# Channel matrices of the later convolution slices completed on chip, and one input gate of the first step pair formed by seven products instead of eight

## The chip, the cores and the metric

The kernel runs on one NeuronCore of a Trainium2 chip. The metric is the device time of one execution in microseconds, as the median of three runs. The kernel is one launch; all five engines (TensorE = PE, VectorE = DVE, ScalarE = ACT, GpSimd = POOL, SyncE = SP) work from queues of their own, and each executes its queue in order.

## The reference, cut to what matters

The whole program is a GRU over 64 steps, a ternary-weight layer, a depthwise convolution over the batch axis and a mixture of experts with a shared expert. Only the GRU's input gates and the convolution are touched.

```python
x: (B=128, T=64, D=512)      cond_2048: (128, 512)
# 1 GRU
gi = x_t @ W_ih + b_ih;  gh = h @ W_hh + b_hh          # each (128, 1536): gates r, z, n
r = sigmoid(i_r + h_r); z = sigmoid(i_z + h_z); n = tanh(i_n + r * h_n)
h = (1 - z) * n + z * h
# 2 x = x + einsum(h, ternary(weight)) + bias
# 3 causal depthwise convolution along the 64 steps, a tap per channel and step, from cond_2048
y = conv(x, taps) + b
# 4 x = x + experts(y) + shared_expert(y)
```

All matrices are float32. Everything after step 3 is the same in both kernels.

## The kernel before

**Order of the work.** The scan of 64 steps comes first (0 to about 1398 us of the profile), then the convolution (about 1398 to 1467 us), then the shared expert with the routing and the experts. A scheduler places each instruction in its engine's queue from the order in which the Python code emits it; where the code needs a fixed order it says so with `in_order` (a chain of VectorE instructions) or `tc.issue_after`.

**Input gates.** `input_gates` is a generator: each `yield` stands for one product of two matmuls (128x256 outputs, contraction 2 x 128), and the scan's loop pulls ten or eleven of them into each step, between the step's recurrent products (`psgh`, line 598) and the turning of the new state. Steps are taken in pairs. For every pair but the first, a gate's two steps are computed by `Chunk` with seven products in place of eight: the operand sums of the pair (`pair_operands`, four GpSimd instructions of 128x256) and the weight sums (`prepare`, four VectorE instructions of 128x512 a gate) allow it, and VectorE adds the partial results with the bias. The third product of a chunk is executed within the following chunk. The first pair (t = 0 and 1) is computed in the plain way by `first_products`: for each gate 2 x 2 blocks for two steps, eight yields, four ScalarE copies out of PSUM. Gates come in the order 0, 2, 1. Their biases are added afterwards by `first_biases`, VectorE instructions in the fixed chain. The products pulled ahead of the first recurrent product are 24 of the first pair, then the turning of the initial state, then three of the second pair.

**Channel matrices.** A slice `sl` of the convolution has 32 channels (two halves `hf` of DS = 16). For each channel the convolution is a matrix of taps: `tz[partition 2s+hf, hf, u, d, t]` holds, for step s, output half u and channel d, the tap `s + 32u + t`. `toeplitz(q)` writes the matrices of one group of 16 channels from `taps` to DRAM (`tzd`) during step q + 2 of the scan, one DMA for each output half: u = 0 has only the 32 steps s = 32 to 63, u = 1 all 64. `load_toeplitz(sl)` brings a slice's matrices to SBUF by four DMAs: two of 64 KB (u = 0) and two of 128 KB (u = 1). For the first NCB = 4 slices SP issues them, within the scan; for slices 4 to 15 GpSimd issues them, within the convolution. There are four `tz` buffers and four `xc` buffers (`sl % NCB`), so the loads of slice sl wait until TensorE has done slice sl - 4.

**Convolution.** Per slice SP also issues two loads of 512 KB of the activations (`load_steps`, `xc<-x1c`). A slice is four groups of eight matmuls (`conv_group`, line 182, 16 records of the profile a group), and VectorE adds the bias while it moves each group to `hid` (line 713, two instructions a group). The last slices are followed by the stores of the expert table and the loads of the shared expert's weights.

Of the kernel before, what the change touches and what calls it, by code (L numbers as in the profile page):

```python
# [8 lines left out]
F32 = mybir.dt.float32  # L9
# [10 lines left out]
P = 128  # L20
# [22 lines left out]
def adaln_ffn_kernel(  # L43
# [22 lines left out]
    nc = tc.nc  # L66
# [8 lines left out]
    tzd = dram.tile([2 * NSL, 2, T, DS, T // 2], F32, name="tzd")  # L75
# [10 lines left out]
        out=before,  # L86
        in_=before,
# [18 lines left out]
    tzs, xcs = [], []  # L106
# [15 lines left out]
    NCB = 4  # L122
# [6 lines left out]
    HALVES = [(0, T // 2), (1, 0)]  # L129

    def toeplitz(q):


        for u, s0 in HALVES:
            i = nc.sync.dma_start(
                out=tzd[q, u, s0:],
                in_=bass.AP(
                    taps.tensor,
                    taps.offset + q * DS * 2 * T + s0 + u * T // 2,
                    [[1, T - s0], [2 * T, DS], [1, T // 2]],  # L140
                ),
            )
            tc.keep_in_program_order(i)

        nc.sync.dma_start(
            out=x1c[q, :TAIL].rearrange("s (r b) e -> (s r) (b e)", r=8), in_=zrow[: 8 * TAIL, : B * DS // 8]
        )

    def load_toeplitz(sl):
        for hf in range(2):
            for u, s0 in HALVES:
                (nc.sync if sl < NCB else nc.gpsimd).dma_start(
                    out=tzs[sl % NCB][2 * s0 + hf :: 2, hf, u], in_=tzd[2 * sl + hf, u, s0:]
                )

    def load_steps(sl, steps):
        for hf in range(2):
# [36 lines left out]
    HK = KD // 2  # L196
    HD = D // 2
    gis_ = ExitStack()
    ps_gi = gis_.enter_context(tc.tile_pool(name="ps_gi", bufs=1, space=PSUM))
    with (  # L200
# [9 lines left out]
        xps, xns = {}, {}  # L210
# [30 lines left out]
        bi = wi.tile([P, 3 * D], F32, name="bi")  # L241
# [12 lines left out]
        cols = [slice(c * D, (c + 1) * D) for c in range(3)]  # L254
# [24 lines left out]
        bh = {}  # L279
# [21 lines left out]
        ps = ps_f.tile([P, D], F32, name="psf")  # L301
# [7 lines left out]
        def prepare(c):  # L309

            w11, w12, w21, w22 = (block(c, k, n) for k in range(2) for n in range(2))
            t1, t2, t4 = (wi.tile([P, HK, HD], F32, name=f"t{n}{c}") for n in (1, 2, 4))
            in_order(nc.vector.tensor_sub, t1, w12, w11)
            in_order(nc.vector.tensor_sub, t2, w22, t1)
            in_order(nc.vector.tensor_sub, w12, w22, w12)
            in_order(nc.vector.tensor_sub, t4, w21, t2)
            wsum[c] = {1: w11, 2: w21, 3: w22, 4: t4, 5: t1, 6: t2, 7: w12}
# [3 lines left out]
        def in_order(op, *operands):  # L321
            with tc.issue_after(summed[-1].ins) if summed else nullcontext():
                summed.append(op(*operands))

        def first_biases(t):
            for c in (0, 2, 1):
                b = bi[:, cols[c]]
                if t == 0 and c in bh:
                    in_order(nc.vector.tensor_add, b, b, bh[c])
                in_order(nc.vector.tensor_add, gis[t, c], gis[t, c], b)  # L330

        def first_products(c, xp):

            for t in range(2):
                gis[t, c] = gip.tile([P, 2, HD], F32, name="gi").rearrange("p h d -> p (h d)")
            accs = {}
            for k in range(2):
                for n in range(2):
                    for t in range(2):
                        if k == 0:  # L340
                            accs[t, n] = ps_gi.tile(
                                [P, D], F32, name={(0, 0): "psx", (1, 0): "psw", (0, 1): "psy", (1, 1): "psz"}[t, n]
                            )[:, :HD]
                        for j in range(HK):
                            i = nc.tensor.matmul(
                                accs[t, n],
                                xp[:, t, k * HK + j, :],
                                block(c, k, n)[:, j, :],
                                start=(k == 0 and j == 0),
                                stop=(k == 1 and j == HK - 1),  # L350
                            )
                        made.append(i)
                        if k == 1:
                            nc.scalar.copy(gis[t, c][:, n * HD : (n + 1) * HD], accs[t, n])
                        yield
# [5 lines left out]
        def pair_operands(t):  # L361

            xp = xps.pop(t)
            x11, x12 = xp[:, 0, :HK], xp[:, 0, HK:]
            x21, x22 = xp[:, 1, :HK], xp[:, 1, HK:]
            s = xpp.tile([P, 3, HK, B], F32, name="xs")
            s1, s2, s4 = s[:, 0], s[:, 1], s[:, 2]
            engine = nc.gpsimd
            engine.tensor_add(s1, x21, x22)
            engine.tensor_sub(s2, s1, x11)  # L370
            engine.tensor_sub(x21, x11, x21)
            engine.tensor_sub(s4, x12, s2)
            return {1: x11, 2: x12, 3: s4, 4: x22, 5: s1, 6: s2, 7: x21}

        class Chunk:


            def __init__(self, t, c, ops):
                self.c, self.ops, self.ws = c, ops, wsum[c]
                self.g = [gip.tile([P, 2, HD], F32, name="gi") for _ in range(2)]  # L380
                gis[t, c], gis[t + 1, c] = (g.rearrange("p h d -> p (h d)") for g in self.g)
                self.ps = {}

            def product(self, n):

                name, first = {
                    1: ("psx", True),
                    2: ("psx", False),
                    6: ("psy", True),
                    7: ("psw", True),  # L390
                    4: ("psw", False),
                    5: ("psz", True),
                    3: ("psz", False),
                }[n]
                if first:
                    self.ps[name] = ps_gi.tile([P, D], F32, name=name)[:, :HD]
                ps = self.ps[name]
                for k in range(HK):
                    i = nc.tensor.matmul(  # L399
                        ps,  # L400
                        self.ops[n][:, k, :],
                        self.ws[n][:, k, :],
                        start=(first and k == 0),
                        stop=(k == HK - 1),
                        skip_group_check=not first,
                    )
                made.append(i)
                g0, g1 = self.g
                add = nc.vector.tensor_add
                both = ps.unsqueeze(1).to_broadcast([P, 2, HD])  # L410
                b = bi[:, cols[self.c]].rearrange("p (h d) -> p h d", h=2)
                if n == 1:
                    self.p1 = gtp.tile([P, 2, HD], F32, name="p1")
                    add(self.p1, both, b)  # L414
                elif n == 6:
                    self.u2 = gtp.tile([P, 2, HD], F32, name="u2")
                    add(self.u2, both, self.p1)
                elif n == 7:
                    self.u3 = gtp.tile([P, HD], F32, name="u3")
                    add(self.u3, ps, self.u2[:, 1])  # L420
                elif n == 5:
                    add(g1[:, 1], ps, self.u3)
                elif n == 2:
                    add(g0[:, 0], ps, b[:, 0])
                elif n == 4:
                    add(g1[:, 0], ps, self.u2[:, 0])
                elif n == 3:
                    add(g0[:, 1], ps, self.u2[:, 1])

        def input_gates():  # L430


            prev = None
            xp = xps.pop(0)
            for c in (0, 2, 1):

                for _ in first_products(c, xp):
                    yield
                if c == 0:
                    prepare(0)  # L440
            prepare(2)
            first_biases(0)
            prepare(1)
            first_biases(1)
            for t in range(2, T, 2):
                ops = pair_operands(t)
                for c in (0, 2, 1):
                    cur = Chunk(t, c, ops)
                    for n in (1, 6, 7, 3, 2, 4, 5):
                        which = prev if n == 3 else cur  # L450
                        if which:
                            which.product(n)
                            yield
                    prev = cur
            prev.product(3)
            yield
# [66 lines left out]

        stream = input_gates()
        load_x(0)
        for _ in range(24):
            next(stream)
        hT = transposed(h)
        for _ in range(3):
            next(stream)  # L530

        def ternary():
# [1131 lines left out]
```

## Time and profile before

| | |
|---|---|
| median of 3 runs | 2639.47 us (2638.37 to 2640.01) |
| the profiled execution's own time | 2639.73 us |
| its span (first to last instruction) | 2637.7 us |
| TensorE busy | 2626.6 us, so idle for 11.1 us of the span |
| VectorE, ScalarE, GpSimd busy | 1403.7, 427.7, 451.4 us |
| granted TensorE clock | 1.0 throughout |
| convolution, 1398 to 1475 us | TensorE busy 72.99 of 77.00 us, DMA engines busy 95%, 319 GB/s |

The profiled execution is 0.26 us over the median of the runs, and 2.03 us of it lie outside its span. The share of busy time of an engine is an average; what bounds a stage is read from that stage: from the windows' table, the gaps of TensorE in its timeline, and the landing times of the transfers.

### The profile page before, as it was taken

The numbers are of one execution on the slowest core, as the hardware profiler recorded it, in microseconds if no ns is written. First come the engines' busy times: TensorE is split into PE (matmuls) and PEld (weight loads), VectorE is DVE, ScalarE is ACT, GpSimd is POOL, SyncE is SP. The second block draws the span as 40 slices with busy tenths as digits, with TensorE's granted clock in tenths as the row PEclk, the third lists the DMA queues.
The fourth block names the chain that finished last, engine by engine and source line by source line (L and its number), as shares of the span: only waits on it lengthen the run. The fifth ranks groups of instructions, "written<-read, shape, count | busy, mean of one in ns | idle before, by whom it ended". The sixth has DMA issues, their size and how long they took to land.

```text
span 2637.7 us, 31178 instructions
## 1 busy us (share of the span) xinstructions
PE 2626.6 (100%) x11993; PEld 1826.7 (69%) x11993; DVE 1403.7 (53%) x3110; ACT 427.7 (16%) x795; POOL 451.4 (17%) x512
## 2 busy tenths in 40 slices
PE   9999999999999999999999999999999999999999
PEld 7666666666666666666668767878877666666667
DVE  6555555555555555555557755666675343333434
ACT  1111111111111111111110222222221111111111
POOL 2111121111111111111113100000001222222220
PEclk9999999999999999999999999999999999999999
DMA  5333232332322222322228831222255999999972
GB/s 197 73 58 66 54 63 59 58 61 54 61 47 52 44 52 44 76 44 52 44 57 278 303 90 21 44 62 63 70 161 158 304 304 283 283 314 301 292 203 50
DMA packets 477492, 323.33 MB, mean 123 GB/s; under 512 B 329056, under 2 KB 397920, under 8 KB 475168
## 3 DMA queue, kind: packets, MB, share of 16 engines
q1 hardware_dynamic: 448880, 248.18, 33.9%
q0 software_dynamic: 28464, 73.16, 11.5%
q8 instruction: 95, 1.56, 0.2%
q14 instruction: 53, 0.43, 0.0%
HBM read 235.01 MB, written 92.55 MB: 124 GB/s over the span
## 4 chain that ended last, share of the span: by engine, by line
PE 99%; DMA 1%; DVE 0%; issue 0%; POOL 0%; ACT 0%; SPq 0%; DVEq 0%
PE psgh L598 25%; PE psw L823 7%; PE psz L823 7%; PE psx L823 7%; PE psz L399 6%; PE psw L399 6%; PE psx L399 6%; PE psf L494 4%; PE y L823 4%; PE py L1549 3%; PE psy L399 3%; PE pg L1523 3%; PE pu L1523 3%; PE y L1000 2%; PE psc L182 1%; PE lg L1151 1%
## 5 line engine op out<-in xcount | busy, mean ns | idle before, releaser
L598 PE MATMUL psgh<-whh,hT 128*128 128x512 f32 x1528 | 671.0, 595 | 0.5 <-ACT hT L471 0.5
L598 PEld LDWEIGHTS psgh<-whh,hT 128*128 128x128 f32 x1528 | 285.2, 190 | 348.5 <-issue 334.6
L399 PE MATMUL psx<-wih,xp 128*128 128x256 f32 x744 | 191.0, 379 | 0.0
L220 POOL DMA_DIRECT2D xn<-in_x_dram x61 | 33.9, 555 | 841.3 <-DVE x L506 828.9
L399 PEld LDWEIGHTS psx<-wih,xp 128*128 128x128 f32 x744 | 138.9, 190 | 18.0 <-issue 0.5
L625 DVE TENSOR_TENSOR n<-psgh,bhn 128x512 f32<-128x512 f32 (+1 forms) x65 | 44.3, 683 | 171.0 <-PE psgh L598 170.9
L1533 DVE SCALAR_TENSOR_TENSOR a<-a,rw,pu 128x352 f32<-128x352 f32 x32 | 18.6, 580 | 213.0 <-PE pu L1523 213.0
L471 ACT COPY hT<-psf 128x512 f32<-128x512 f32 x63 | 37.0, 587 | 556.5 <-PE psf L463 556.4
L609 DVE TENSOR_TENSOR r<-psgh,gi 128x512 f32<-128x512 f32 x64 | 44.3, 692 | 141.2 <-PE psgh L598 141.2
L1105 POOL DMA_DIRECT2D out_dram<-hid x32 | 27.6, 1010 | 449.8 <-issue 332.9
L490 POOL TENSOR_TENSOR xn<-xn,fb 128x512 f32<-128x512 f32 x61 | 77.0, 1263 | 143.7 <-DMA xn<-in_x_dram 143.7
L399 PE MATMUL psz<-wih,xs 128*128 128x256 f32 x372 | 95.6, 379 | 0.1
L399 PE MATMUL psw<-t,xp 128*128 128x256 f32 x372 | 95.6, 379 | 0.0
L399 PE MATMUL psy<-t,xs 128*128 128x256 f32 x372 | 95.5, 379 | 0.0
L399 PE MATMUL psz<-t,xs 128*128 128x256 f32 x372 | 95.5, 379 | 0.0
L494 PE MATMUL psf<-sgn,hhi 128*128 128x512 f32 x256 | 95.1, 493 | 0.3 <-DVE hlo L479 0.3
L399 PE MATMUL psw<-wih,xp 128*128 128x256 f32 x372 | 95.4, 379 | 0.0
L1549 PE MATMUL py<-wd,aeT 128*64 128x512 f32 (+1 forms) x384 | 88.8, 597 | 0.0
L628 ACT ACTIVATE n<-n 128x512 f32<-128x512 f32 (+1 forms) x65 | 40.4, 623 | 276.7 <-DVE n L627 276.7
L414 DVE TENSOR_TENSOR p<-psx,bi 128x512 f32<-128x512 f32 x93 | 64.4, 692 | 36.9 <-PE psx L399 36.9
L1523 PE MATMUL pg<-wg,xeT 128*64 128x352 f32 x512 | 81.2, 459 | 0.0
L1523 PE MATMUL pu<-wu,xeT 128*64 128x352 f32 x512 | 81.2, 459 | 0.0
(350 smaller groups left out, 4760.2 us busy)
## 6 DMA issues: line engine op xcount, KB each, us to landing
wg<-in_w_gate_dram SPq DMA_DIRECT2D x64, 704.0 KB, 12.5
wu<-in_w_up_dram SPq DMA_DIRECT2D x64, 704.0 KB, 12.6
wd<-in_w_down_dram SPq DMA_DIRECT2D x64, 512.0 KB, 9.8
x1c<-x SPq DMA_DIRECT2D x62, 256.0 KB, 5.2
out_dram<-x SPq DMA_DIRECT2D x62, 256.0 KB, 5.4
xn<-in_x_dram POOLq DMA_DIRECT2D x61, 256.0 KB, 4.1
xp<-in_xT_dram POOLq DMA_DIRECT2D x30, 512.0 KB, 5.2
xc<-x1c SPq DMA_DIRECT2D x28, 512.0 KB, 8.6
```

The lines of the kernel that those rows point to most:

```text
L399: i = nc.tensor.matmul(ps, self.ops[n][:, k, :], self.ws[n][:, k, :], start=(first and k == 0), stop=(k == HK - 1), skip_group_check=not f ...
L414: add(self.p1, both, b)
L490: nc.gpsimd.tensor_add(xn, xn, fb)
L494: nc.tensor.matmul(ps, piece[:, k, :], sgn[:, k, :], start=(i == 0 and k == 0), stop=(i == 1 and k == KD - 1),)
L598: nc.tensor.matmul(ps[:, piece], hT[:, k, :], whh[c][:, k, piece], start=(k == 0), stop=(k == KD - 1),)
L609: i = nc.vector.tensor_add(r, ps_r, gis.pop((t, 0)))
L625: nc.vector.tensor_add(n[:, p], ps_n[:, p], bhn[:, p])
L628: nc.scalar.activation(n[:, p], n[:, p], AF.Tanh)
L823: i = nc.tensor.matmul(ps.rearrange("p (j b) -> p j b", b=P) if len(r.shape) == 3 else ps, lhs(k), r, start=(first and k == 0), stop=(k == ...
L1000: nc.tensor.matmul(gu.rearrange("p (j b) -> p j b", b=P), swr[:, k].rearrange("p w n -> p (w n)"), rows[:, k], start=(k == 0), stop=(k == ...
L1523: nc.tensor.matmul(acc[halves[j]], self.xeT[:, k, halves[j]], self.ws[j][which][:, k, :], start=(k == 0), stop=(k == KD - 1),)
L1549: nc.tensor.matmul(py[halves[j]], self.aeT[:n, c, halves[j]], self.ws[j][2][:n, c, :], start=(c == 0), stop=(c == len(ech) - 1),)
```

## The change

It has two parts.

**First part.** The matrix of u = 0 on partitions 64 to 127 (steps 32 to 63) equals that of u = 1 on partitions 0 to 63 (steps 0 to 31). For slices 4 to 15 the u = 0 half is no longer written to `tzd` (24 DMAs of SP less in the scan) and no longer loaded (24 DMAs of GpSimd less in the convolution). In its place ScalarE copies it within the buffer, 64 partitions x 1024 elements, once a slice.

**Second part.** Gate 1 of the first pair is computed by a `Chunk` of seven products, with operand sums by GpSimd for pair 0. The chunk leaves its biases out (`biased=False`): product 1 and product 2 leave PSUM by ScalarE copies, and `first_biases` adds all biases of the first pair once the chunk's product 3 is done. Since the plain products of the two other gates still need x21, the operand `x11 - x21` of pair 0 goes to a buffer of its own. `prepare(1)` moves ahead of `prepare(2)`. Ahead of the first recurrent product there are now 22 products, the turning of the initial state, and four products.

```diff
     def toeplitz(q):
-        for u, s0 in HALVES:
+        for u, s0 in HALVES if q < 2 * NCB else HALVES[1:]:
...
     def load_toeplitz(sl):
+        tz = tzs[sl % NCB]
         for hf in range(2):
             for u, s0 in HALVES:
-                (nc.sync if sl < NCB else nc.gpsimd).dma_start(
-                    out=tzs[sl % NCB][2 * s0 + hf :: 2, hf, u], in_=tzd[2 * sl + hf, u, s0:]
-                )
+                if sl < NCB or u:
+                    (nc.sync if sl < NCB else nc.gpsimd).dma_start(
+                        out=tz[2 * s0 + hf :: 2, hf, u], in_=tzd[2 * sl + hf, u, s0:]
+                    )
+        if sl >= NCB:
+            nc.scalar.copy(tz[P // 2 :, :, 0], tz[: P // 2, :, 1])
...
         def first_biases(t):
             for c in (0, 2, 1):
-                b = bi[:, cols[c]]
-                if t == 0 and c in bh:
-                    in_order(nc.vector.tensor_add, b, b, bh[c])
-                in_order(nc.vector.tensor_add, gis[t, c], gis[t, c], b)
+                in_order(nc.vector.tensor_add, gis[t, c], gis[t, c], bi[:, cols[c]])
...
+            s7 = x21 if t else gtp.tile([P, 2, HD], F32, name="p1")[:, 0].rearrange(
+                "p (k b) -> p k b", k=HK
+            )
-            engine.tensor_sub(x21, x11, x21)
+            engine.tensor_sub(s7, x11, x21)
...
                 if n == 1:
                     self.p1 = gtp.tile([P, 2, HD], F32, name="p1")
-                    add(self.p1, both, b)
+                    if self.biased:
+                        add(self.p1, both, b)
+                    else:
+                        for h_ in range(2):
+                            nc.scalar.copy(self.p1[:, h_], ps)
...
+                elif n == 2 and not self.biased:
+                    nc.scalar.copy(g0[:, 0], ps)
...
         def input_gates():
             prev = None
-            xp = xps.pop(0)
-            for c in (0, 2, 1):
+            xp = xps[0]
+            ops = pair_operands(0)
+            for c in (0, 2):
                 for _ in first_products(c, xp):
                     yield
                 if c == 0:
                     prepare(0)
+                    prepare(1)
+            cur = Chunk(0, 1, ops, False)
+            for n in (1, 6, 7, 2, 4, 5):
+                cur.product(n)
+                yield
+            prev = cur
             prepare(2)
-            first_biases(0)
-            prepare(1)
-            first_biases(1)
+            for c in (0, 1):
+                in_order(nc.vector.tensor_add, bi[:, cols[c]], bi[:, cols[c]], bh[c])
...
                             which.product(n)
+                            if not which.biased and n == 3:
+                                for t_ in range(2):
+                                    first_biases(t_)
                             yield
...
-        for _ in range(24):
+        for _ in range(22):
             next(stream)
         hT = transposed(h)
-        for _ in range(3):
+        for _ in range(4):
             next(stream)
```

More of the change, by code (lines that the diff above doesn't have):

```diff
@@ L368, in pair_operands, with __init__ @@
             engine = nc.gpsimd
+            s7 = x21 if t else gtp.tile([P, 2, HD], F32, name="p1")[:, 0].rearrange(
+                "p (k b) -> p k b", k=HK
+            )
             engine.tensor_add(s1, x21, x22)
             engine.tensor_sub(s2, s1, x11)
-            engine.tensor_sub(x21, x11, x21)
+            engine.tensor_sub(s7, x11, x21)
             engine.tensor_sub(s4, x12, s2)
-            return {1: x11, 2: x12, 3: s4, 4: x22, 5: s1, 6: s2, 7: x21}
+            return {1: x11, 2: x12, 3: s4, 4: x22, 5: s1, 6: s2, 7: s7}
         class Chunk:
-            def __init__(self, t, c, ops):
+            def __init__(self, t, c, ops, biased=True):
+                self.biased = biased
                 self.c, self.ops, self.ws = c, ops, wsum[c]
```

## The prediction

> **What bounds the kernel now.** I read the engines' shares first, then the chain of work that ended last, then TensorE's waits, and only then the two stages that the change touches. The page's first part and the chain say that the whole kernel runs at TensorE's pace:
>
> ```profile
> PE 2626.6 (100%) x11993; PEld 1826.7 (69%) x11993; DVE 1403.7 (53%) x3110; ACT 427.7 (16%) x795; POOL 451.4 (17%) x512
> PE 99%; DMA 1%; DVE 0%; issue 0%; POOL 0%; ACT 0%; SPq 0%; DVEq 0%
> ```
>
> [...]a gain can come only from work taken off it, from its 11.1 us of gaps (2637.7 - 2626.6), or from matmuls that run slower than their neighbours. From 60 to 1000 us it has no gap at all (940.00 us busy in 940), so the 24 DMAs that SP no longer issues in the scan buy nothing there. The gaps lie in the first 27 us (1.5 us) and in the convolution (4.0 us in 77):
>
> ```profile
> 0.00:27.00 27.00, 25.53 (x115) 22.32 (x116) 9.99 (x15) 5.78 (x13) 9.70 (x18) 1.00 0.94 332
> 60.00:1000.00 940.00, 940.00 (x3378) 621.31 (x3378) 511.92 (x892) 134.38 (x217) 163.34 (x197) 1.00 0.29 56
> 1398.00:1475.00 77.00, 72.99 (x1084) 67.52 (x1084) 59.81 (x157) 1.62 (x5) 33.46 (x63) 1.00 0.95 319
> 1423.00:1442.00 19.00, 18.07 (x306) 17.67 (x305) 15.73 (x45) 0.00 (x0) 9.60 (x18) 1.00 1.02 339
> ```
>
> The columns are busy us of PE, PEld, DVE, ACT and POOL, then clock, DMA share, GB/s. From 1423 us on the DMA engines are full, while ScalarE does nothing: the stage has two owners, and its second half belongs to the transfers. TensorE's own timeline shows it, a slice being 64 records:
>
> ```profile
> 1436.86 3.96 PE L182 MATMUL psc<-tz,xc 128*64 128x128 f32 x64 [0.43 <-DMA tz<-tzd]
> 1441.32 8.01 PE L182 MATMUL psc<-tz,xc 128*64 128x128 f32 x128 [0.50 <-DMA tz<-tzd]
> 1449.66 8.05 PE L182 MATMUL psc<-tz,xc 128*64 128x128 f32 x128 [0.33 <-PE psc L182]
> 1458.18 7.70 PE L182 MATMUL psc<-tz,xc 128*64 128x128 f32 x128 [0.47 <-DVE hid L713]
> ```
>
> Counting records, slices 4 to 7 start at 1417.62, 1421.31, 1425.00 and 1428.66, a pace of 3.68 us; slices 9 to 15 start at 1436.86, 1441.32, 1445.35, 1449.66, 1453.72, 1458.18 and 1461.94, a pace of 4.18. Each of slices 9 to 14 starts 0.3 to 0.5 us after its last `tz` transfer has landed, and its last `xc` transfer lands only 0.3 to 0.7 us before that (slice 12: xc 1448.65, tz 1449.20, start 1449.66). So the landings set the pace. The issues on GpSimd show a second brake:
>
> ```profile
> 1429.18 0.53 POOL L154 DMA_DIRECT2D tz<-tzd  x1 [1.17 <-PE psc L182]
> 1430.33 0.55 POOL L154 DMA_DIRECT2D tz<-tzd  x1 [0.62 <-DMA tz<-tzd]
> 1431.25 0.53 POOL L154 DMA_DIRECT2D tz<-tzd  x1 [0.36 <-DMA tz<-tzd]
> 1432.31 0.55 POOL L154 DMA_DIRECT2D tz<-tzd  x1 [0.53 <-DMA tz<-tzd]
> ```
>
> GpSimd's DMAs take eight semaphores in turn, so each issue waits until the eighth before it has landed (slice 8's third landed at 1430.96, slice 10's third is issued at 1431.25). With four DMAs a slice, each some 8 us in flight, that allows one slice per 4.2 us, just the pace of the bytes.
>
> In the start-up the plain products of gate 1 follow each other without a gap:
>
> ```profile
> 19.47 1.03 PE L345 MATMUL psx<-wih,xp 128*128 128x256 f32 x4
> 25.51 1.03 PE L345 MATMUL psz<-wih,xp 128*128 128x256 f32 x4
> 16.57 0.92 POOL L369 TENSOR_TENSOR xs<-xp 128x256 f32<-128x256 f32 x1 [10.60 <-DMA xp<-in_xT_dram]
> 23.70 0.69 DVE L323 TENSOR_TENSOR bi<-bi,r 128x512 f32<-128x512 f32 x1 [1.27 <-DMA r<-in_b_hh_dram]
> 33.04 0.69 DVE L609 TENSOR_TENSOR r<-psgh,gi 128x512 f32<-128x512 f32 x1
> ```
>
> Seven intervals in 25.51 - 19.47 = 6.04 us: a product is 0.863 us of TensorE.
>
> [...]a slice's last `xc` (SP) and last `tz` (GpSimd) land within 0.7 us of each other; fewer `tz` bytes should therefore speed `xc` too. [...]
>
> ```profile
> L471 ACT COPY hT<-psf 128x512 f32<-128x512 f32 x63 | 37.0, 587 | 556.5 <-PE psf L463 556.4
> L852 ACT COPY u<-psx 128x256 f32<-128x256 f32 x80 | 29.7, 371 | 70.1 <-PE psx L823 69.8 <-PE psb L1373 0.3
> ```
>
> **The change part by part. Start-up.** One product less on TensorE, nowhere given back: 24 + 3 products stood ahead of the first recurrent one, now 22 + 4, and the rest of TensorE's queue is the same. That is -0.86 us, if nothing stalls. What must be ready: product 6 of the new chunk, due near 19.47 + 0.86 = 20.3 us, needs GpSimd's sums of pair 0 and `prepare(1)`. GpSimd's four instructions (0.92 to 1.17 us each as for pair 2, about 4.2 us) come ahead of and between the two memsets of 1.8 us; pair 0's operands have landed before 8 us, since products read them, so this ends by about 15. `prepare(1)` needs gate 1's weights; they stand in SP's queue ahead of pair 2's operands, which GpSimd waited for until 16.57, so I put them at 14.5 us. Four VectorE steps of 0.69, slowed to as much as 1.22 beside GpSimd, end by 18. Behind them in VectorE's queue stand `prepare(2)` (four more, to about 20.6) and a bias sum (to 21.4); only then does VectorE add product 6 and, at about 22.2, product 7, whose PSUM tile product 4 overwrites near 22.7. The margin is some 0.1 us, so I give back 0.1, at most 0.9. The second bias sum waits for its row until 23.70; product 5's addition behind it is due at 24.4. ScalarE copies twice after product 1 (2 x 0.37 us) in place of one VectorE addition, and once after product 2, where it had four copies before: nothing. The six additions of `first_biases` (6 x 0.69 = 4.1 us), of which four now come after product 3 (near 28.3), end near 31.6; the addition at line 609 was due at 33.04 and is now due at 32.2. After it the state has some 5 us until TensorE turns it. Sum: -0.8 us, from -0.86 to 0.
>
> **Convolution.** A slice's loads shrink from 2 x 512 + 2 x 128 + 2 x 64 = 1408 KB (1.442 MB) to 1280 KB (1.311 MB), 9% less. At 1.442 MB per 4.2 us = 343 GB/s the new pace of the transfers is 3.82 us; in slices 5 to 9, where landings were 4.5 us apart, 4.1. TensorE's pace is 3.68. GpSimd issues two DMAs a slice, so eight semaphores cover four slices and that wait is gone. The new step: ScalarE's copy, 1024 elements at (587 - 371)/256 = 0.84 ns plus a fixed 0.16, is 1.0 us, with some 0.3 for two signals (TensorE's lag behind a landing above). Half the partitions are written and the source is SBUF, not PSUM, which no row shows; bounds 0.6 us (if only half the lanes' work counts) and 2.1 (twice). Nothing else stands in ScalarE's queue from 1402 to 1462 us, so the copy waits for its transfers alone; behind it only the next copies, then line 731's, due 1462.
>
> Slack: in slice 5 the last landing was at 1418.09, the start at 1421.31, so 3.2 us. Fewer bytes in slices 4 and 5 add 0.7, the copy takes 1.3: 2.6. It shrinks by 4.1 - 3.68 = 0.4 a slice up to slice 10 (0.5 left) and by 0.14 after that, to about zero at slice 15. So TensorE would hold its own pace: slices 4 to 15 took 1461.94 - 1417.62 = 44.3 us for 11 intervals, and 11 x 3.68 = 40.5 is 3.8 less. For late landings at the end I keep 0.4: -3.4 us. VectorE, 4 x 0.76 + 0.23 = 3.3 us a slice, stays below TensorE. Late next are VectorE's last additions, which held the first turned block back by 0.94 us and still do; the shared expert's weights are released by the slices and queue behind fewer bytes, so they move ahead as well.
>
> Sum: -0.8 - 3.4 = -4.2 against the profiled 2639.73, whose own time is 0.26 over the median: 2635.5 there and 2635.3 as a median.
>
> **The rivals.** *Slower, by the extra hop.* If a landing takes its time for reasons other than bytes (latency of many transfers at once), the copy makes each slice's ready time later. Between a release and the start of the slice four later lie 3 slices of TensorE; in slices 9 to 14 release to last landing took 11.0 to 11.7 us. With landings as before, 1.3 us more in a loop of four slices is 0.33 a slice, over eleven 3.6: 2639.5 - 0.8 + 3.6 = 2642.3. It decides from the point where landings shorten by less than 1.3 us. Against it: with the engines at 102%, landing time is queueing.
> *The transfers stay the bound.* If two `xc` loads set the rate and removed `tz` bytes count little, the pace stays near 4.1: conv gains 11 x 0.08 or so, in all -1.7: 2637.8. For it: `xc` lands as late as `tz`.
> *More than the sum.* All of the convolution's gaps go and no start-up margin is lost, the remaining 0.3 to 0.9 us gaps at its two ends as well: -0.86 - 3.8 - 1 = 2633.8.
> *The start-up stalls.* VectorE's queue order costs the 0.9 us: 2636.1. That the change doesn't do what it says is excluded: the built program has twelve copies and two DMAs a slice.
>
> **How the numbers follow.** Forecast 0.55, transfers or start-up partly in the way 0.25, extra hop 0.10, more than the sum 0.10. A measurement of this kernel tells about 0.2% (5.3 us) from no change. The forecast lies inside; faster than 2634.2 are the last case and a sixth of the first, 0.2; slower than 2644.7 only the extra hop with a copy of 2.1 us, 0.05; 0.75 remain. The range 2633.0 to 2640.0 leaves out the worst of both ends.
>
> **What would show it right or wrong.** Right: slices 9 to 15 start 3.7 us apart; line 154's waits for a landing are gone; twelve ScalarE copies of about 1.0 us that end before TensorE needs them; first recurrent product at 28.5 instead of 29.40 us. Wrong: TensorE waits for ScalarE in the convolution, slices stay 4.1 us or more apart, or a gap stands between products 7 and 4 near 22 us.

## The result and the profile after

| | before | after |
|---|---|---|
| median | 2639.28 us (22 runs, 2638.31 to 2642.18) | 2635.78 us (22 runs, 2634.79 to 2637.47) |
| ratio after/before | | 0.9987, 95% interval 0.9981 to 0.9993 |
| profiled execution's own time, span | 2639.73, 2637.7 us | 2635.61, 2633.8 us |
| first recurrent product starts at | 29.40 us | 28.61 us |
| convolution's products (`psc`, slices 1 to 15) | 1406.27 to 1465.88: 59.62 us | 1405.43 to 1461.49: 56.06 us |
| slices 9 to 15, start to start | 4.18 us | 3.71 us |

The kernel became 3.5 us faster in the median and 4.1 us in the profiled pair (3.9 us of it in the span). The interval leaves out 1, but a change of 0.13% is small, so the trace has to show where it lies. On the page of after, the first part and the chain say the same as before. TensorE is busy for 1.9 us less, and the four records fewer are the product that was left out:

```profile
PE 2624.7 (100%) x11989; PEld 1826.1 (69%) x11989; DVE 1405.8 (53%) x3115; ACT 439.7 (17%) x806; POOL 441.6 (17%) x492
PE 99%; DVE 0%; issue 0%; ACT 0%; DVEq 0%
```

The windows' table of after, for the stretches shown of before (busy us of PE, PEld, DVE, ACT, POOL, then clock, DMA share, GB/s):

```profile
0.00:27.00 27.00, 25.87 (x115) 22.79 (x116) 14.62 (x22) 6.92 (x14) 13.43 (x22) 1.00 0.94 330
60.00:1000.00 940.00, 940.00 (x3381) 621.80 (x3380) 513.89 (x892) 133.75 (x216) 163.53 (x197) 1.00 0.28 55
1398.00:1475.00 77.00, 74.89 (x1097) 69.59 (x1094) 62.02 (x164) 18.09 (x22) 20.36 (x39) 1.00 0.90 323
1423.00:1442.00 19.00, 19.00 (x333) 19.00 (x332) 16.16 (x47) 5.23 (x5) 5.32 (x10) 1.00 0.98 357
```

From 1423 us on TensorE is now busy for all 19.00 us where it had 18.07, and ScalarE has its five copies there. TensorE's timeline of after has one line for all 15 slices, where before had a new one for every slice or two from slice 9 on: there is no gap between the first and the last of the 960 records. (Slice 0 runs ahead of them, into other PSUM tiles.) The wait of 0.94 us ahead of the first turned block (`pst`) stayed:

```profile
1405.43 56.06 PE L189 MATMUL psc<-tz,xc 128*64 128x128 f32 x960 [0.91 <-DVE xl L530]
1462.43 1.06 PE L1151 MATMUL pst<-ident,hid 128*128 128x128 f32 x8 [0.94 <-DVE hid L737]
```

The copies, in ScalarE's timeline and as a tile's group (duration in ns as least/median/most), and GpSimd's issues:

```profile
1423.98 1.05 ACT L163 COPY tz<-tz 64x1024 f32<-64x1024 f32 x1 [1.81 <-DMA tz<-tzd]
1427.52 1.04 ACT L163 COPY tz<-tz 64x1024 f32<-64x1024 f32 x1 [2.49 <-DMA tz<-tzd]
```

```profile
L163 ACT COPY tz<-tz x12: 1044/1046/1050, 1408.2 to 1454.6; 64x1024 f32<-64x1024 f32 x12
```

```profile
1424.92 1.06 POOL L157 DMA_DIRECT2D tz<-tzd  x2 [2.63 <-issue]
1428.60 1.07 POOL L157 DMA_DIRECT2D tz<-tzd  x2 [2.62 <-ACT tz L163]
1432.29 1.06 POOL L157 DMA_DIRECT2D tz<-tzd  x2 [2.62 <-issue]
```

Two issues a slice, none waiting for a landing. Each copy ends 1.8 to 3.0 us before TensorE starts its slice (slices 8 to 15).

In the start-up, product 4 of the new chunk (`psw`, at 22.89 in TensorE's timeline) takes 1.12 us instead of 1.03. VectorE's timeline shows why: the addition of product 7 (line 433), whose PSUM tile product 4 overwrites, ran only at 22.40, behind that of product 6 and the bias sum:

```profile
22.03 1.03 PE L408 MATMUL psx<-wih,xp 128*128 128x256 f32 x4
22.89 1.12 PE L408 MATMUL psw<-t,xp 128*128 128x256 f32 x4
23.85 1.03 PE L408 MATMUL psz<-t,xs 128*128 128x256 f32 x4
```

```profile
20.49 1.21 DVE L330 TENSOR_TENSOR bi<-bi,r 128x512 f32<-128x512 f32 x1
21.62 0.68 DVE L430 TENSOR_TENSOR u<-psy,p 128x512 f32<-128x512 f32 x1
22.40 0.42 DVE L433 TENSOR_TENSOR u<-psw,u 128x256 f32<-128x256 f32 x1
```

The interval from product 4 to 5 is 0.96 us instead of 0.86.

### The profile page after: what moved, and what is told of

It reads as the page before. It is cut to its first block, busy times and chain, and to the rows that moved or that the text cites. A ratio compares the mean times of both kernels' runs of the same rounds, so it can differ in the third digit from the quotient of the medians.

```text
span 2633.8 us, 31154 instructions
## 1 busy us (share of the span) xinstructions
PE 2624.7 (100%) x11989; PEld 1826.1 (69%) x11989; DVE 1405.8 (53%) x3115; ACT 439.7 (17%) x806; POOL 441.6 (17%) x492
## 4 chain that ended last, share of the span: by engine, by line
PE 99%; DVE 0%; issue 0%; ACT 0%; DVEq 0%
PE psgh L622 25%; PE psw L847 7%; PE psz L847 7%; PE psx L847 7%; PE psz L408 6%; PE psw L408 6%; PE psx L408 6%; PE psf L518 4%; PE y L847 4%; PE py L1573 3%; PE psy L408 3%; PE pg L1547 3%; PE pu L1547 3%; PE y L1024 2%; PE psc L189 2%; PE lg L1175 1%
## 5 line engine op out<-in xcount | busy, mean ns | idle before, releaser
L634 ACT ACTIVATE r<-r 128x512 f32<-128x512 f32 x64 | 40.3, 630 | 249.3 <-DVE r L633 249.3
```

## The experiments

All times are against runs of before on the same chip. "Stretch" is the time of the convolution's products (slices 1 to 15), "pace" the mean distance of the starts of slices 9 to 15. One profile is one execution: the stretches of before and of e2, whose convolutions are the same, are 0.65 us apart. The work behind the convolution differs as well. It took 1172.3 to 1174.0 us in the seven profiles whose slices come in two loads of 128 KB with the copy behind them (after, e1, e4, e7 to e10), and 1171.4 to 1171.9 us in the seven others. So it isn't chance alone; the cause is open. For the questions below the stretch tells more than the span or the median.

### The two parts alone

**e1_copy_only** is before with the first part alone, **e2_gates_only** before with the second alone.

```diff
# e1_copy_only, against before
-        for u, s0 in HALVES:
+        for u, s0 in HALVES if q < 2 * NCB else HALVES[1:]:
...
+                if sl < NCB or u:
...
+        if sl >= NCB:
+            nc.scalar.copy(tz[P // 2 :, :, 0], tz[: P // 2, :, 1])
# e2_gates_only, against after: toeplitz and load_toeplitz as in before
```

> The kernel before with the first part alone: ScalarE completes the channel matrices of slices 4 to 15; the first pair's gates stay plain. Theory (the parts add up, and the convolution holds nearly all of the gain): slices 5 to 15 start 3.7 us apart, the convolution's psc products end 3.5 us sooner than before relative to their start, the first recurrent product starts at 29.4 us as before; 2635.9 to 2636.2 as against 2639.3 before. Rival (the gain comes from the start-up, or the parts help each other): less than 2 us in the convolution, time above 2637.3.

> The kernel before with the second part alone: gate 1 of the first pair by seven products; all four matrix loads as before. Theory: one product of 0.86 us less and 0.1 us lost to VectorE's queue, first recurrent product 0.8 us sooner (28.6 us), convolution as before with slices 9 to 15 4.2 us apart; 2638.5, which a timing of five rounds can hardly tell from no change. Rival (an earlier scan lets the convolution's transfers start ahead and changes more): more than 1.5 us.

The copy alone: 2636.68 us, ratio 0.9988 (0.9981 to 0.9994), stretch 56.11, pace 3.71. The gate alone: 2638.73 us, ratio 0.9996 (0.9987 to 1.0004), first recurrent product at 28.55, stretch 60.27, pace 4.27. So the parts add up: the convolution's gain is the first part's, and the second part's 0.8 us are in the trace, but its interval contains 1.

### Why the transfers became fast enough

The prediction took bytes at 343 GB/s for the limit. **e3_two_wide** has no copy and *more* bytes: each half's u = 0 and u = 1 matrices in one load of 256 KB (the 32 missing rows of u = 0 are zeros), two DMAs a slice, 1536 KB with the activations. **e5_four_wide** moves the same bytes in four loads of 128 KB.

```diff
# e3_two_wide, against after (slices 4 to 15); copy removed, u = 0 written whole
+                nc.gpsimd.dma_start(
+                    out=tzs[sl % NCB][hf::2, hf].rearrange("s u d t -> s u (d t)"),
+                    in_=tzd[2 * sl + hf].rearrange("u s d t -> s u (d t)"),
+                )
# e5_four_wide, against e2: four loads, of all 64 rows each; u = 0 written whole, as in e3
-            for u, s0 in HALVES:
+            for u, s0 in HALVES if sl < NCB else ((0, 0), (1, 0)):
```

> The second part as in the changed kernel, no copies: for slices 4 to 15 GpSimd loads each half's whole matrix, both output halves and all 64 steps, in one DMA of 256 KB. Per slice two DMAs instead of four, but 1536 KB instead of 1408 (the added rows are zeros). It sets the two brakes against each other. Theory of the bytes: the pace of the slices is bytes over 343 GB/s, 1.573 MB gives 4.6 us, so slices 9 to 15 start 4.5 to 4.6 us apart and the convolution is 3 to 5 us longer than before; 2641 to 2644. Rival, theory of the eight semaphores (a ninth DMA waits for the first): with two DMAs a slice that wait is gone, slices start 3.7 to 3.9 us apart, 2635 to 2637.

> As the run with two whole-half loads of 256 KB a slice (1536 KB in all, no copies), but each split by output half: four DMAs of 128 KB a slice, 64 rows each. Bytes, rows and descriptors are the same, only the number of DMAs differs. Theory of the eight semaphores: a landing of 8 to 9.8 us allows a slice per 4 x 8/8 = 4.0 to 4.9 us, so slices 9 to 15 start 4.1 to 4.9 us apart, GpSimd waits for landings again, the psc stretch takes 60 to 64 us (57.0 with two DMAs), time 2639 to 2643. Rival (what slowed the kernel before was the shape of the 64 KB loads, which reach only partitions 64 to 127): 3.8 us apart, 57 us, 2636.

e3: 2635.90 us, ratio 0.9986 (0.9979 to 0.9993), stretch 57.02, pace 3.86. With 9% more bytes than before it is as fast as after in the median, so the theory of bytes fell at once. e5: 2638.04 us, ratio 0.9994 (0.9985 to 1.0002), stretch 58.99, pace 3.82, which lies between its two expectations. GpSimd waited for landings 15 times (8.7 us in all); slices 7, 8 and 9 started 4.76, 4.38 and 4.37 us after the one before, and the later ones 3.7 to 4.1. With the bytes of e3 in twice as many loads the stretch is 2.0 us longer, so the number of loads counts too, but it doesn't give before's steady pace of 4.18. The DMA view from 1424 to 1446 us, of before and of e3:

```profile
DMA packets 1668, 7.49 MB, mean 340 GB/s; under 512 B 501, under 2 KB 501, under 8 KB 1013
...
xc<-x1c SPq DMA_DIRECT2D x12, 512.0 KB, 10.1
tz<-tzd POOLq DMA_DIRECT2D x10, 128.0 KB, 8.2
tz<-tzd POOLq DMA_DIRECT2D x10, 64.0 KB, 8.1
```

```profile
DMA packets 1822, 8.93 MB, mean 406 GB/s; under 512 B 367, under 2 KB 367, under 8 KB 1100
```

The engines were full in both (busy share 1.03 and 1.02), yet moved 340 or 406 GB/s, so a busy share of 1 doesn't say that they move the most they can.

What else differs between the loads? Before's u = 0 loads write partitions 64 to 127 only; the other loads of these slices are spread over all 128. **e6_four_small** is after with each 128 KB load split in two of 64 KB, one for partitions 0 to 63, one for 64 to 127. **e11_four_spread** splits it so that each takes every fourth partition of all 128: same number, same bytes.

```diff
# e6_four_small, against after: each load of slices 4 to 15 in two
+                    for r in range(2):
+                        nc.gpsimd.dma_start(
+                            out=tz[r * T + hf : (r + 1) * T : 2, hf, u],
+                            in_=tzd[2 * sl + hf, u, r * T // 2 : (r + 1) * T // 2],
+                        )
# e11_four_spread: the same with
+                            out=tz[2 * r + hf :: 4, hf, u],
+                            in_=tzd[2 * sl + hf, u, r::2],
```

> The changed kernel with its copies, each of the two 128 KB loads of a slice split by rows into two of 64 KB: 1280 KB as in the changed kernel, but four DMAs. Theory of the eight semaphores: they bind only when a landing is over 8/4 of a slice's time, 7.4 us; with 5.9 us as in the changed kernel they don't, so slices stay 3.7 us apart and the psc stretch at 56 to 57 us, 2635.5 to 2636.5. Rival (four DMAs a slice are slow in themselves, whatever their bytes): 4.1 us apart, 59.5 us, 2639.

> As e6 (each 128 KB load of after in two loads of 64 KB, four DMAs a slice, 1280 KB), but each of the two covers every fourth partition, over all 128, rather than one half of the partitions. Rival A (which partitions a load reaches decides its rate): 350 GB/s or more from 1424 to 1446 us, stretch 56.0 to 56.7. Rival B (the number of loads and of rows in each decides, wherever they lie): as e6, 310 to 330 GB/s, stretch 57.3 to 57.7. The time between them isn't told apart by the median: 2635.8 against 2637.3.

e6: 2637.32 us, ratio 0.9991 (0.9982 to 1.0), stretch 57.46, between its two expectations; slices 11 to 14 start 4.07, 3.90 and 4.47 us apart. e11: 2635.31 us, ratio 0.9983 (0.9977 to 0.999), stretch 56.08, pace 3.70, like after. The DMA view of the same window, e6, then e11:

```profile
DMA packets 1550, 6.95 MB, mean 316 GB/s; under 512 B 525, under 2 KB 525, under 8 KB 883
...
tz<-tzd POOLq DMA_DIRECT2D x24, 64.0 KB, 7.4
```

```profile
DMA packets 1691, 7.71 MB, mean 350 GB/s; under 512 B 565, under 2 KB 565, under 8 KB 941
...
tz<-tzd POOLq DMA_DIRECT2D x24, 64.0 KB, 6.3
```

The median landing falls from 7.4 to 6.3 us by the choice of rows alone. But a row's place in SBUF and its place in DRAM go together here: e6's loads read one block of DRAM each, e11's every second row of 2 KB. Which of the two sides makes the difference, no run here separates. (350 GB/s is no limit: 1.311 MB a slice at TensorE's 3.7 us is 354.) **e12_same_bytes** then gives the kernel after the very traffic of before, two loads of 128 and two of 64 KB, 1408 KB a slice, but with the small ones on every fourth partition.

```diff
# e12_same_bytes, against after (toeplitz writes the whole u = 0 half again)
+                else:
+                    nc.gpsimd.dma_start(out=tz[hf::4, hf, u], in_=tzd[2 * sl + hf, u, ::2])
```

> The loads of before in number and bytes (per slice two of 128 KB and two of 64 KB by GpSimd, 1408 KB with the activations), in the kernel after, copy included; but the two loads of 64 KB lie on every fourth of all 128 partitions (the even steps; the copy then overwrites what has to be the other half) instead of on partitions 64 to 127. The later slices' whole u = 0 matrices are written to DRAM for it, within the scan. Theory (loads that land on one half of the partitions are what slowed the transfers of before; e6 against e11): 360 GB/s or more from 1424 to 1446 us, pace of slices 9 to 15 of 3.7 to 3.8 us, stretch 56.1 to 57.2. Rival A (bytes): 343 GB/s, pace 4.2, stretch 60 or more. Rival B (four DMAs through eight semaphores, whatever their rate): pace 4.0 to 4.2, 58.5 to 60.

2635.47 us, ratio 0.9982 (0.9976 to 0.9989), stretch 57.34, pace 3.93. The rate is the theory's; stretch and pace are a little above its ranges and below those of both rivals. In the DMA view:

```profile
DMA packets 1850, 8.39 MB, mean 382 GB/s; under 512 B 552, under 2 KB 552, under 8 KB 1103
...
tz<-tzd POOLq DMA_DIRECT2D x11, 128.0 KB, 6.8
tz<-tzd POOLq DMA_DIRECT2D x12, 64.0 KB, 6.6
```

That is 382 GB/s in place of 340, and the loads land 1.4 to 1.5 us sooner after their issue than before's. From slice 9 on, slices start 3.7 to 3.8 us apart except for one, which came 1.2 us late behind loads that took some 8 us to land; TensorE's timeline has that one gap, and its cause is open:

```profile
1405.48 37.56 PE L191 MATMUL psc<-tz,xc 128*64 128x128 f32 x640 [0.91 <-DVE xl L532]
1444.02 18.80 PE L191 MATMUL psc<-tz,xc 128*64 128x128 f32 x320 [0.98 <-DMA tz<-tzd]
```

So with the same bytes and the same number of loads, 2.3 of the 3.56 us (59.62 - 57.34) come back by which rows the small loads carry. The rest, at most 1.3 us, is one late slice, and belongs to bytes, number of loads or chance. The medians, 2635.47 us here and 2635.78 for after, show no loss against after. Rival B, that four loads are slow whatever their rate, fell likewise: in GpSimd's waits over the whole convolution, before and e12 (us in total, times, longest), the waits for the eighth-last landing (in before each of the 23 issues from 1430.33 to 1453.66 us came 0.28 to 0.53 us after it) nearly vanish with the landing times:

```profile
POOL tz L154 <- DMA tz<-tzd: 11.5, 23, 0.8
```

```profile
POOL tz L157 <- DMA tz<-tzd: 1.9, 3, 1.0
POOL tz L161 <- DMA tz<-tzd: 0.5, 2, 0.3
```

### Is the copy's hop really paid out of slack?

The copy is one more step, a "hop", between a load's landing and the products. **e7_copy_x4** and **e10_copy_x3** make the copy four and three times over, **e8_copy_dve** puts it on VectorE.

```diff
# e7_copy_x4, against after (e10_copy_x3: range(3))
+            for _ in range(4):
+                nc.scalar.copy(tz[P // 2 :, :, 0], tz[: P // 2, :, 1])
# e8_copy_dve, against after
-            nc.scalar.copy(tz[P // 2 :, :, 0], tz[: P // 2, :, 1])
+            nc.vector.tensor_copy(tz[P // 2 :, :, 0], tz[: P // 2, :, 1])
```

> The changed kernel with each ScalarE copy made four times over (the same values): the hop is 4 x 1.05 = 4.2 us instead of 1.05. It prices the slack of 1.8 to 3.0 us that lies between a copy's end and its slice. Theory: 3.14 us more uses the slack up and then delays a loop of four slices by what is left (0.1 to 1.3 us), 0.2 a slice; psc stretch 57 to 59 us, 1 to 3 us slower than the changed kernel. Rival (the hop is on the path from the first microsecond): a quarter of 3.14 us a slice, 0.79, 8.6 us in eleven slices; 2644.

> ScalarE's copy of the later slices made three times over (same values). 3 x 1.05 = 3.14 us a slice stays under TensorE's 3.7, unlike the four copies of e7, so ScalarE can't set the pace; what is added is 2.1 us between landing and start. Theory (the copies of after are ready 1.8 to 3.0 us early, so the hop is paid out of slack): convolution's product stretch 56.1 to 57.0 us, pace 3.7 to 3.75. Rival (extra hop closes the loop release - load - copy - start, 2.1 us over four slices, 0.5 us a slice): pace 4.0 to 4.2, stretch 60 to 62.

> The changed kernel with the copy on VectorE instead of ScalarE. VectorE has 4 x 0.76 + 0.23 = 3.3 us of work in a slice of 3.7, and its queue is in order: a copy of 0.5 to 1.1 us that waits for a landing holds up the additions behind it. Theory: VectorE becomes the bound, 3.9 to 4.4 us a slice, psc stretch 59 to 64 us, 3 to 8 us slower than the changed kernel. Rival (the copy fits into VectorE's gaps): as the changed kernel within 1 us.

e7 missed both expectations: 2641.60 us, ratio 1.0008 (0.9999 to 1.0017), stretch 61.75, pace 4.19. That is 4 x 1.046 = 4.18: ScalarE itself had become the bound (from 1423.32 us on its timeline has 21 copies in 21.98 us), which I had not counted. TensorE's waits in e7 (us in total, times, longest):

```profile
PE psc L190 <- ACT tz L164: 2.6, 9, 1.1
```

e10 repeats the question below that bound: 3 x 1.046 = 3.14 us a slice, 2.1 us more between landing and start. Stretch 56.21, pace 3.73, no wait of TensorE for ScalarE; 2637.10 us, ratio 0.999 (0.9981 to 0.9999). The slack swallows the hop, and would have swallowed three of it. (The median's 1.3 us over after's don't lie in the convolution, whose stretch is 0.15 us longer; the work behind it is 1.4 us longer in the profiles.)

e8 had the right direction and far too small a size: 2660.82 us, ratio 1.0077 (1.0059 to 1.0095), stretch 82.29, pace 6.38. VectorE needs only 0.69 us for the copy, but waits for the landing with TensorE's additions queued behind:

```profile
1435.24 0.69 DVE L163 COPY tz<-tz 64x1024 f32<-64x1024 f32 x1 [3.58 <-DMA tz<-tzd]
1435.95 2.08 DVE L737 TENSOR_TENSOR hid<-psc,cb 128x256 f32<-128x256 f32 x6
```

Six additions (PSUM tiles that TensorE needs) stand behind that wait; TensorE stops (up to 1475 us it waited for them 16.0 us, 5 times), the buffer is released later, the next load starts later (GpSimd waited for TensorE's products 47.0 us, 10 times, ahead of such loads; in after 9.2 us, 3 times), and the wait feeds itself (the copies waited for landings 19.9 us, 8 times). TensorE's gaps between these products are 16.8 us. They aren't all of the 26.2 us that the stretch grew: in e8 alone the granted clock fell within the convolution, to 0.50 for 3.4 to 6.8 us, five times, 20.5 us in all. Each time began within one of the five gaps of 2.5 to 4.5 us or up to 1.3 us behind it. The products were then 0.106 us apart instead of 0.058; for the 163 of them that is an estimate of some 8 us (163 x 0.048). Two of these times in the windows' table (columns as above):

```profile
1424.53:1427.94 3.41, 3.06 (x30) 3.10 (x32) 2.69 (x9) 0.00 (x0) 0.00 (x0) 0.50 0.61 245
1472.32:1479.14 6.82, 4.38 (x42) 4.41 (x44) 4.98 (x14) 0.00 (x0) 0.00 (x0) 0.50 0.36 94
```

ScalarE is the better place although its copy is half as long again (1.046 us for 0.69), because nothing is queued behind it: stretch 56.06 in after, 82.29 here.

### Could a second gate be had?

**e4_two_gates** is after with gate 2 of the first pair by seven products too; **e9_two_gates_late** hands the weight sums of the following gate to VectorE only after product 7 of the running one.

```diff
# e4_two_gates, against after
+            for c in (2, 1, 0):
+                prepare(c)
+            for c in (2, 1):
+                cur = Chunk(0, c, ops, False)
...
-        for _ in range(22):
+        for _ in range(21):
# e9_two_gates_late, against e4: prepare(2) alone stays ahead, and in the loop
+                    if n == 7:
+                        prepare(c - 1)
```

> The changed kernel, with gates 2 and 1 of the first pair both by seven products (gate 0 plain), VectorE's weight sums in the order 2, 1, 0, and x11 - x21 in place again. Theory: a further product of 0.86 us less on TensorE, first recurrent product at 27.75 us, the rest as in the changed kernel; 0.7 to 0.9 us below it, some 2634.9. Rival (VectorE's or GpSimd's queue holds TensorE up, since weight sums and operand sums are due 6 us sooner): gaps of TensorE between 12 and 24 us eat it, no gain or up to 1 us lost.

> Both gates 2 and 1 of the first pair by seven products (as e4), but the weight sums of the following gate are handed to VectorE only after product 7 of the running gate. Theory (e4's missing gain was VectorE's in-order queue, the weight sums standing ahead of the additions): the second saved product shows, first recurrent product at 27.7 to 28.0 us (after: 28.61; e4: 29.24), no wait of TensorE for the u addition of more than 0.2 us. Rival (the seven-product form itself needs more VectorE work than eight products leave room for, whatever the order): first recurrent product at 28.6 or later, TensorE waits for gi or u for 0.5 us or more. In the median of runs at most 0.9 us below after, which this measurement can't tell from no change.

The first weights arrive at different times in different executions (the fourth product starts between 7.4 and 8.6 us in the profiles of this study), so I count from there. From the fourth product to the first recurrent one it is 21.16 us in before, 20.40 in after, 21.21 in e4 and 20.54 in e9. Neither gains on after: 2637.82 us, ratio 0.9992 (0.9984 to 1.0), and 2636.84 us, ratio 0.9989 (0.9983 to 0.9996). The later order takes away one of e4's two waits and leaves the other. In both runs the theory fell and the rival's signs came: TensorE waits for VectorE, and the first recurrent product starts at 29.24 and 28.61 us. TensorE's waits, e4, then e9:

```profile
PE psw L406 <- DVE u L431: 0.8, 1, 0.8
PE psw L406 <- DVE gi L439: 0.4, 1, 0.4
```

```profile
PE psw L406 <- DVE u L431: 0.8, 1, 0.8
```

In VectorE's timeline of e9 there is no idle time from 15 to 23.7 us, and the weight sums beside GpSimd's sums of pair 2 (16.30 to 20.1 us) take 1.2 us instead of 0.68:

```profile
17.66 1.21 DVE L330 TENSOR_TENSOR t<-wih,wih 128x512 f32<-128x512 f32 x1
...
21.82 0.68 DVE L330 TENSOR_TENSOR t<-wih,t 128x512 f32<-128x512 f32 x1
22.42 0.41 DVE L431 TENSOR_TENSOR u<-psw,u 128x256 f32<-128x256 f32 x1
```

VectorE is full in this stretch: the seven-product form trades 0.86 us of TensorE for VectorE's time, and as far as these two orders show, the first gate took what there was.

## Why the prediction was right, point by point

**The sum.** -4.2 us was forecast for the profiled execution, -4.12 came; 2635.3 as a median, 2635.78 came. The agreement is closer than the working deserves: start-up and convolution gave 4.35, some 0.5 went back behind them, and 0.2 lie outside the span.

**Start-up: right to 0.1 us.** -0.79 for -0.8, and -0.76 counted from the fourth product. Each step stood where it was put: the stall of 0.1 us at product 4, the addition of product 7 at 22.40 (put at 22.2), line 633's at 32.24 (put at 32.2). That it is 0.1 us is in part luck: with the same start-up, product 4 waited for VectorE for 0.3 us in e3 and e8, where the first weights had come earlier, and the interval from the fourth product was 20.8 us instead of 20.3 to 20.4. So the rival of a stalled start-up is there, and it is small. e2 shows the saving alone, and e4 and e9 that the margin really was the last one.

**Convolution: the size right, the reason wrong.** -3.56 for -3.4. The landings did set the pace, but the step from there to bytes failed: "At 1.442 MB per 4.2 us = 343 GB/s the new pace of the transfers is 3.82 us". e3 and e12 moved 406 and 382 GB/s in the same place, so "with the engines at 102%, landing time is queueing" doesn't hold either. By e11 and e12 against e6 and before, most of what held before back was the shape of two of the four loads a slice, which write one half of the partitions (from one block of DRAM); the change removes just these. How much their number and bytes add is open, within the 1.3 us that e12 leaves. Three of the prediction's statements fell with it. The new pace of the transfers isn't 3.82 to 4.1 us: after runs at TensorE's own 3.71. The slack didn't shrink to zero at slice 15: 1.9 us were left there, 1.8 at the least (slice 10). And the second brake, eight semaphores, isn't a brake of its own: e11 and e12 have as many DMAs as before and go at 3.7 to 3.8 but for one slice. It is the landing time that makes it bind (estimates from the median landings: 4 x 8.1 / 8 = 4.1 us a slice before, 4 x 6.3 / 8 = 3.2 in e11), as it did for a few slices in e5. The sum held all the same, because TensorE's pace, the other end of the step, was read from the profile and not from a rate; any cause that freed the transfers gave the same number. In this the size was luck: it didn't test the reason.

**The copy: right.** 1.046 us for 1.0. e10 shows the hop paid out of slack.

**The rivals.** The extra hop, the only rival by which the kernel gets slower, needs landings shortened by less than 1.3 us; they shortened by 2.3 (`tz`, 8.2 to 5.9). Transfers that stay the bound would have shown a pace near 4.1. Of "more than the sum" the gaps inside the convolution did go, but those at its two ends stayed (0.91 and 0.94 us).

**What was left out.** That the shared expert's weights "move ahead as well" held: their two large loads land 4.7 us earlier (1469.38 to 1464.64 and 1472.72 to 1468.04), though they take 1.4 to 1.5 us longer from issue to landing. But the prediction gave nothing back behind the convolution, and some of the gain went there. At the first turned block after is 4.40 us ahead of before (1466.82 to 1462.43), at 1485 us 4.20, at the end of the span 3.9. Of the first 0.2 us the trace shows a candidate: the memset that waits for the table's stores holds VectorE 3.38 instead of 2.81 us. The other 0.3 come near the end, and their cause is open. Other profiles with after's loads lose more there (some 2 us against before in e4).

## What to carry to other kernels

Before a transfer stage is priced by its bytes, look at where each load writes: here the small loads that reach half of the partitions went with slow landings of the others beside them (8.2 us for the 128 KB loads of before, 6.8 in e12), and spreading their rows, or replacing them by an on-chip copy, was worth more than their bytes (2.3 of the 3.56 us). A DMA share of 1 is no proof of a limit (340 GB/s at 1.03 in before, 406 at 1.02 in e3); a variant with more bytes in a better shape tests it in one run. Put a copy that waits for a landing on an engine whose queue holds nothing else, even if another engine is faster at it (1.046 us on ScalarE and a stretch of 56.06, 0.69 on VectorE and 82.29).

## What the hardware showed that I had not expected

- The same 16 DMA engines at a busy share of 0.99 to 1.03 moved between 316 GB/s (e6, loads on half of the partitions) and 406 GB/s (e3).
- An SBUF copy of 64x1024 float32 from partitions 0 to 63 to 64 to 127 took 1.046 us on ScalarE, 0.69 us on VectorE.
- Queued ahead of other work, the faster copy cost 26.2 us of stretch (82.29 against 56.06), though its twelve executions are 4.3 us shorter in all (12 x (1.046 - 0.69)).
- TensorE's gaps of 2.5 to 4.5 us in e8 each went with a granted clock of 0.50 for 3.4 to 6.8 us. Its waits of up to 1.1 us in the convolution of e7 did not: the clock stayed at 1.0 there.
